# Seven block products for batch 13 of a fused cross-attention kernel, with its statistics later and the loads of x one pair of steps later

## The chip, the cores and the metric

The kernel runs on one core of one Trainium2 chip. The metric is the device time of one execution in microseconds (us), as the median of several runs. All arithmetic is in float32.

## The reference, cut to what matters

There are 16 batches. Each has 256 rows of `x` (256 numbers wide, two tiles of 128 rows) and 77 context rows (192 wide). There are 8 heads of 256.

```
Q = x @ Wq ; K = ctx @ Wk ; V = ctx @ Wv            (8 heads of 256)
score = Q K^T / 16, masked ; attn = softmax(score)   (256 x 77 a head)
out   = concat(attn V) @ Wo + x
return layernorm(out) * gamma + beta                 (over 256 columns)
```

## The kernel before, in words

The kernel never forms Q, K and V. It first multiplies the weights together (`Wk Wq^T` a head into `gA`, `gB`, and `Wv Wo` a head into `uA`, `uB`). For each group of 4 batches it then makes `a` (context times `gA`, `gB`; `prepare_a`, L157) and for each batch `vw` (context times `uA`, `uB`; `prepare_vw`, L205). The scores of a tile are one product of turned `x` with `a`; the output is one product of the turned softmax weights with `vw`.

The work after the start is a hand-written loop over steps `b` from -1 to 14 (L937). Each engine does its instructions strictly in the order in which the code issues them; there is no scheduler. **Step b** holds

- `scores` (L282, TensorE) of the two tiles of batch b+1, then `shift` (L298, VectorE: 16 instructions that add the mask and take the maximum), `exponential` (L318, ScalarE: 16 exponentials), `weigh` (L334, VectorE reciprocal, then GpSimd multiplies into `p`) and `turn` (L352, VectorE transposes `p` into `pT`);
- the output products of batch b;
- the statistics (`finish`, L485: mean and variance on VectorE; `spread`, L507: the inverse root on ScalarE) and the normalisation (`normalise`, L540) of batch b-1, called `old`, and its store. With `aside` the normalisation goes to ScalarE (L546) and GpSimd (L547, L548), and a small GpSimd instruction `less` (L523) goes ahead of it; otherwise it is two VectorE instructions (L533, L552);
- `prepare_vw` and `prepare_a` for later batches, whose results ScalarE copies out of PSUM (L923). Up to step 10 an odd step does this for two batches (a long step, `ahead`) and an even step not at all. From step 11 on every step does it for one.

Tile t belongs to batch t // 2, so tiles 26 and 27 are batch 13.

The output products exist in two forms. `attend` (L362) is eight blocks and a ninth for the last 13 keys, for each tile. `seven(b)` (L421) does the two tiles of a batch at once with seven block products in place of eight (Strassen's scheme in Winograd's form). It needs `differences(b)` (L394: one GpSimd instruction over 768 columns, `ts`) and `sums(b)` (L406: four GpSimd instructions, `ss`, each on the one before or on `pT`), a copy of `pm` to `m` on ScalarE (L459), and afterwards `add_seven(b)` (L462): two additions of `po` to `x` on VectorE (L483) and five additions on GpSimd (L469). `NS` says how many batches take this form: 13 in this kernel, so batches 0 to 12.

The loads are issued by SyncE (SP), also in order: a store waits for its normalisation, and what stands behind it waits too. In odd steps up to 9, `load_x` (L118) brings four tiles of `x` (512 KB, `xg`) and `load_xT` (L144) brings the same four tiles in a blocked order in four transfers of 128 KB (`xT`). Before they are used, `transpose_x` (L154) turns `xT` in place, in two VectorE instructions for four tiles. Here these instructions stand in step b+2 when the loads stand in step b. In an even step the second tile's normalisation is put `behind` and comes in the next step after `shift` and ahead of the loads.

The PSUM has eight banks, taken in turn.

Of the kernel before, what the change touches and what calls it, by code (L numbers as in the profile page):

```python
# [16 lines left out]
P = 128  # L17
# [10 lines left out]
def kernel(  # L28
# [53 lines left out]
    NH = DI // 2 // BK  # L82
    uA = const.tile([P, 5, NH, NF, BK], F32, tag="uA", name="uA")
    uB = const.tile([P, 5, NH, NF, BK], F32, tag="uB", name="uB")
    NS = B - GB // 2 - 1

    def of_e(u, e):
        return u[:, 3 - 2 * e : 5 - 2 * e].rearrange("p q n i c -> p (q n) i c")
# [25 lines left out]
    def load_x(g, n=None, of=QT):  # L114
        if not n:
            xg_of[g] = const.tile([P, GT, DI], F32, tag=f"xg{g}", name=f"xg_{g}")
        lo, hi = (0, GT) if n is None else (n * QT, n * QT + of)
        nc.sync.dma_start(xg_of[g][:, lo:hi], x_rows[:, g * GT + lo : g * GT + hi, :])  # L118
# [3 lines left out]
    def evacuate(dst, src):  # L122
# [3 lines left out]
        else:  # L126
            nc.vector.tensor_copy(dst, src)


    pools = {}  # L130
    xT_of, a_of, vw_of, p_of, mv_of = {}, {}, {}, {}, {}
# [19 lines left out]
    def transpose_x(g, j):  # L151

        cols = xT_of[g][:, j * NM : (j + 2) * NM]
        nc.vector.transpose(cols, cols)  # L154
# [163 lines left out]
    def exponential(t):  # L318
        e = sp.tile([P, H, S2], F32, tag="e", name=f"e_{t}")
        s, top = s_of.pop(t)  # L320
        den = st.tile([P, H], F32, tag="den", name=f"den_{t}")
        for h in range(H):
            one = slice(h, h + 1)
            nc.scalar.activation(  # L324
                e[:, h],
                s[:, h],
                AF.Exp,
                bias=top[:, one],
                scale=-1.0,
                accum_out=den[:, one] if t < QT * NS else None,  # L330
            )
        e_of[t] = e, den

    def weigh(t):  # L334
        e, den = e_of.pop(t)
        if t >= QT * NS:
            nc.vector.tensor_reduce(den, e, AX.X, ALU.add)
        rden = st.tile([P, H], F32, tag="rden", name=f"rden_{t}")
        nc.vector.reciprocal(rden, den)  # L339
        p = p_ring[t % 2]  # L340
        e_mh = e.rearrange("p (m h) k -> p m h k", h=2)
        rden_mh = rden.rearrange("p (m h) -> p m h", h=2)
        for cols, keys in ((slice(2 * KM), slice(KM)), (slice(2 * KM, 2 * S2), slice(KM, None))):
            part = p[:, :, cols].rearrange("p m (h k) -> p m h k", h=2)
            nc.gpsimd.tensor_tensor(  # L345
                part,
                e_mh[:, :, :, keys],
                rden_mh.unsqueeze(3).to_broadcast(list(part.shape)),
                ALU.mult,
            )  # L350

    def turn(t):  # L352
        p = p_ring[t % 2]
        pT_of[t] = turned.tile([P, NF + 1, NM, BK], F32, tag="pT", name=f"pT_{t}", bufs=4)
        nc.vector.transpose(  # L355
            pT_of[t].rearrange("p n m q -> p m n q"),
            p.rearrange("p m (n k) -> p m n k", k=BK),
        )
# [181 lines left out]
    def normalise(t, aside=False, centred=False):  # L540

        g, j = t // GT, t % GT
        rstd, less = rstd_of.pop(t)
        y = xg_of[g][:, j, :]
        if aside:
            nc.scalar.activation(y, y, AF.Identity, bias=less, scale=rstd)  # L546
            nc.gpsimd.tensor_tensor(y, y, gam, ALU.mult)  # L547
            nc.gpsimd.tensor_tensor(y, y, bet, ALU.add)  # L548
        else:
            if not centred:  # L550
                centre(t)
            nc.vector.scalar_tensor_tensor(y, y, rstd, bet, ALU.mult, ALU.add)  # L552
        if t >= NT - 5 * QT:
            store(t)
            return
        done.append(t)
        if t ^ 1 in done:
            t |= 1
            j |= 1
            nc.sync.dma_start(  # L560
                out_rows[:, t + 1 - QT : t + 1, :], xg_of[g][:, j + 1 - QT : j + 1, :]
            )
# [15 lines left out]
    with tc.tile_pool(name="wonce", bufs=1) as wp:  # L578
# [59 lines left out]
            load_blocks(wvT[:, a], wv_blocks[a])  # L638
        for a in range(NF):
            nc.sync.dma_start(wo_of[a // 2][:, a % 2], wo_rows[a])  # L640
        mask_row = mask.rearrange("b k -> (b k)")

        def load_bias(lo, hi):
            nc.sync.dma_start(
                bias_f[:, lo * S2 : hi * S2].bitcast(I32),
                mask_row[lo * S2 : hi * S2].partition_broadcast(P),
            )

        load_xT(0, 0, GT // 2)
        load_bias(0, GB)  # L650
        load_rest()
        load_xT(0, GT // 2, GT)
        load_bias(GB, B)


        idle = ps_mm.tile([P, P], F32, tag="mm", name="idle")
# [194 lines left out]
        for i in range(3):  # L851
            turn_v(i)
        a_of_pairs(2, 3)
        load_x(0)
        nc.sync.dma_start(gam, gamma.partition_broadcast(P))
        nc.sync.dma_start(bet, beta.partition_broadcast(P))
        turn_v(3)
# [52 lines left out]
    def work_of(b, rest_first=False):  # L910
        g, n = b // GB + 1, b % GB
        work = [prepare_vw(b, rest_first)]
        if g < NG - 1 or g == NG - 1 and n < NF // 2:
            work.append(prepare_a(g, (n,), rest_first=rest_first))
        elif b <= NS:
            part = (0, 2) if g < NG else (2, GB)
            work.append(prepare_a(NG - 1, (NF // 2 + n % 2,), *part, rest_first))
        return work
# [5 lines left out]

    behind = []

    def turn_x_and_normalise(g, n, old):
        to_turn = (g, 0) if g < NG and n == 2 else (g - 1, GT // 2) if g > 1 and n == 0 else None
        if to_turn:
            for j in range(to_turn[1], to_turn[1] + GT // 2, 2):  # L930
                transpose_x(to_turn[0], j)
        if old:
            normalise(old[1])

    assert QT == 2
    last = NT - 1
    for b in range(-1, B - 1):  # L937
        old = range(max(b - 1, 0) * QT, b * QT)
        now = range(max(b, 0) * QT, (b + 1) * QT)
        new = range((b + 1) * QT, (b + 2) * QT)  # L940
        for t in new if b >= 0 else ():
            scores(t)
        if b == B - 2:
            for t in old:
                finish(t)
            spread(old[0], old[-1] + 1)
            invert(old[0], old[-1] + 1, aside=old)
            for t in old:
                normalise(t, aside=True)
        for t in new if b >= 0 else ():  # L950
            shift(t)
        while behind:
            behind.pop(0)()
        g, n = (b + 1) // GB + 1, (b + 1) % GB
        if g < NG and n % 2 == 0:
            load_x(g, n, 2 * QT)
            load_xT(g, n * QT, (n + 2) * QT)
        for m in range(0, 2) if b < 0 else range(b + 2, min(b + 3, B // 2)):
            turn_last(m)
        alone = b + 1 >= B - GB  # L960
        works = work_of(b + 1) if alone or n % 2 == 0 else []
        for part_A, _, _ in works:
            part_A()
        for _, part_B, _ in works:
            part_B()
        for i, t in enumerate(new if b >= 0 else ()):
            exponential(t)
            if old and b < B - 2:
                finish(old[i])
            weigh(t)  # L970
        ahead = works and not alone
        if old and b < B - 2 and not ahead:
            spread(old[0], old[-1] + 1)
        if ahead:
            copy_out(works)
            if old:
                spread(old[0], old[-1] + 1)
            works = work_of(b + 2, rest_first=True)
            for _, part_B, _ in works:
                part_B()  # L980
            for part_A, _, _ in works:
                part_A()
        copy_out(works)
        if b + 1 < NS:
            differences(b + 1)
        if b < NS:
            if now:
                seven(b)
            if old:
                invert(old[0], old[-1] + 1)  # L990
                normalise(old[0])
            for t in new:
                turn(t)
            if b < 0:
                for j in range(GT // 2, GT, 2):
                    transpose_x(0, j)
                bias_of(GB, B)
            if alone or ahead:
                turn_x_and_normalise(g, n, old)
            else:  # L1000
                behind.append(partial(turn_x_and_normalise, g, n, old))
            if ahead:
                sums(b + 1)
            if now:
                add_seven(b)
            if b + 1 < NS and not ahead:
                sums(b + 1)
            continue
        for t in now:
            attend(t)  # L1010
        if b < B - 2:
            invert(old[0], old[-1] + 1, aside=old[:1])
            normalise(old[0], aside=True)
            turn(new[0])
            normalise(old[1])
            turn(new[1])
            for t in now:
                add_product(t)
        else:
            turn(new[0])  # L1020
            finish(now[0])
            spread(now[0], now[1])
            turn(new[1])


    attend(last - 1)
# [54 lines left out]
```

## Time and profile before

| what | us |
|---|---|
| median of 3 runs (lowest, highest) | 272.82 (272.69, 273.63) |
| the profiled execution's own time | 272.17 |
| its span in the profile | 270.3 |
| TensorE (PE) busy | 263.6 |
| VectorE (DVE) busy | 185.6 |
| GpSimd (POOL) busy | 171.4 |
| ScalarE (ACT) busy | 155.6 |

The profiled execution lies 0.65 us under the median, and 1.87 us of its time lie outside the span. In the rows below the columns are the start in us, the duration, the engine, the source line and operation, what it writes and reads, and how many instructions were merged; a bracket gives the idle time of the engine before it and what ended it. PEld are TensorE's weight loads, SPq is the queue on which SyncE issues DMAs. The granted clock of TensorE is 1.0 over the whole span after the first microseconds.

Where the steps lie: TensorE begins the scores of step 9 at 188.4, of step 10 at 205.1, of step 11 at 213.2, of step 12 at 225.8, of step 13 at 238.4 and of step 14 at 249.8.

### The profile page before, as it was taken

The page shows a single profiled execution, that of the slowest core. Times are in us where ns is not written, and L with a number is a line of the kernel's source. Part 1 is how long each engine was busy: PE and PEld are TensorE (multiplying, and loading weights), DVE is VectorE, ACT ScalarE, POOL GpSimd, SP SyncE. Part 2 cuts the span into 40 slices and gives each one's busy share as a digit, 9 for nine tenths or more (in the row PEclk, how much of TensorE's full clock was granted, in tenths as well). Part 3 has the DMA queues.
Part 4 walks back from the last instruction along what each step waited for, and adds up shares of the span by engine and source line. Part 5 has one row for each costly group of instructions (what it writes and reads, how often), then busy time and mean ns, then how long its engine had stood idle before and what let it go on. Part 6 is the DMA issues. An engine that isn't in the chain of part 4 may idle for free.

```text
span 270.3 us, 14362 instructions
## 1 busy us (share of the span) xinstructions
PE 263.6 (98%) x6104; PEld 190.5 (70%) x6104; DVE 185.6 (69%) x808; ACT 155.6 (58%) x652; POOL 171.4 (63%) x231
## 2 busy tenths in 40 slices
PE   7999999999999999999999999999999999999993
PEld 6557588754894599449954996489769969684662
DVE  0555938583464858863796479646977898988765
ACT  3233325835858555964687377729584592945752
POOL 1000005726389757996699759964999798966654
PEclk9999999999999999999999999999999999999999
DMA  6998999993000010261016100910091010110102
GB/s 194 203 202 187 327 173 164 309 191 52 2 5 5 2 42 5 75 125 44 2 51 151 41 6 7 191 45 4 7 189 51 2 45 4 44 41 2 62 22 81
DMA packets 42512, 22.69 MB, mean 84 GB/s; under 512 B 23680, under 2 KB 41680, under 8 KB 42448
## 3 DMA queue, kind: packets, MB, share of 16 engines
q1 hardware_dynamic: 42448, 21.77, 37.3%
q8 instruction: 48, 0.79, 1.3%
q14 instruction: 16, 0.13, 0.2%
HBM read 17.57 MB, written 4.19 MB: 81 GB/s over the span
## 4 chain that ended last, share of the span: by engine, by line
PE 91%; DMA 5%; SPq 2%; DVE 1%; issue 0%; DVEq 0%
PE ps L289 25%; PE pa L180 11%; PE pv L214 11%; PE po L434 10%; PE pm L434 9%; PE pv L225 6%; PE pa L192 5%; DMA wk_blk<-in_L_xattn_Wk_dram 5%; PE po L367 4%; PE pu L737 3%; PE pr L248 2%; PE pgb L797 1%; PE pw L751 1%; PE pr L260 1%; SPq L596 1%; PE po L383 1%
## 5 line engine op out<-in xcount | busy, mean ns | idle before, releaser
L324 ACT ACTIVATE e<-s,top 128x77 f32<-128x77 f32 x256 | 83.8, 346 | 46.6 <-DVE top L306 42.6
L289 PE MATMUL ps<-a,xT 128*32 128x154 f32 x2048 | 69.9, 294 | 0.0
L289 PEld LDWEIGHTS ps<-a,xT 128*32 128x32 f32 x2048 | 66.2, 110 | 1.2 <-ACT uB L886 0.4
L345 POOL TENSOR_TENSOR p<-e,rden 128x512 f32<-128x512 f32 x64 | 47.7, 772 | 24.1 <-DVE rden L339 24.1
L306 DVE CUSTOM_DVE_ANT_0 s<-ps,bias 128x77 f32<-128x77 f32 x256 | 43.5, 232 | 15.3 <-PE ps L289 15.3
L324 ACT ACTIVATION_READ_ACCUMULATOR e<-s,top 128x1 f32 x208 | 38.9, 187 | 0.0
L180 PE MATMUL pa<-cA,gA 128*32 128x308 f32 (+1 forms) x576 | 36.4, 394 | 0.0
L469 POOL TENSOR_TENSOR xg<-xg,m 128x256 f32<-128x256 f32 x39 | 28.7, 737 | 7.8 <-DVE xg L483 5.8
L180 PEld LDWEIGHTS pa<-cA,gA 128*32 128x32 f32 x576 | 18.4, 110 | 20.2 <-issue 7.0
L214 PE MATMUL pv<-uA,cA 128*32 128x512 f32 x256 | 30.6, 595 | 0.0
L552 DVE SCALAR_TENSOR_TENSOR xg<-xg,rstd,bet 128x256 f32<-128x256 f32 x26 | 21.2, 816 | 12.8 <-ACT rstd L513 11.5
L398 POOL TENSOR_TENSOR ts<-vw 128x768 f32<-128x768 f32 x13 | 24.0, 1849 | 7.9 <-ACT vw L923 7.9
L355 DVE STREAM_TRANSPOSE pT<-p 128x640 f32<-128x640 f32 x32 | 25.7, 822 | 3.2 <-POOL p L345 3.1
L923 ACT COPY vw<-pv 128x512 f32<-128x512 f32 x32 | 17.7, 584 | 14.7 <-PE pv L214 7.7
L306 DVE DVE_READ_ACCUMULATOR2_ANT top<- 128x1 f32 x256 | 20.8, 81 | 0.0
L483 DVE TENSOR_TENSOR xg<-po,xg 128x256 f32<-128x256 f32 x31 | 11.6, 407 | 13.4 <-PE po L434 12.4
L192 PE MATMUL pa<-cB,gB 64*32 64x308 f32 (+1 forms) x576 | 20.3, 392 | 0.0
L572 POOL TENSOR_TENSOR nan<-nan 128x4 f32<-128x4 f32 (+1 forms) x2 | 0.4, 203 | 31.0 <-DVE nan L571 31.0
L923 ACT COPY a<-pa 128x308 f32<-128x308 f32 (+1 forms) x56 | 18.9, 399 | 1.7 <-PE pa L180 0.2
L192 PEld LDWEIGHTS pa<-cB,gB 64*32 64x32 f32 x576 | 10.7, 107 | 12.3 <-issue 7.5
L225 PE MATMUL pv<-uB,cB 64*32 64x512 f32 x256 | 17.3, 597 | 0.0
L533 DVE SCALAR_TENSOR_TENSOR xg<-xg,mv,gam 128x256 f32<-128x256 f32 x27 | 16.7, 619 | 0.1
(118 smaller groups left out, 409.4 us busy)
## 6 DMA issues: line engine op xcount, KB each, us to landing
xT<-in_x_dram SPq DMA_DIRECT2D x32, 128.0 KB, 5.8
xg<-in_x_dram SPq DMA_DIRECT2D x6, 512.0 KB, 5.0
out_dram<-xg SPq DMA_DIRECT2D x11, 256.0 KB, 2.5
wo<-in_L_xattn_Wo_dram SPq DMA_DIRECT2D x4, 512.0 KB, 6.0
wq_blk<-in_L_xattn_Wq_dram SPq DMA_DIRECT2D x12, 128.0 KB, 4.5
wvT<-in_L_xattn_Wv_dram SPq DMA_DIRECT2D x16, 96.0 KB, 3.4
out_dram<-xg SPq DMA_DIRECT2D x10, 128.0 KB, 2.0
wk_blk<-in_L_xattn_Wk_dram SPq DMA_DIRECT2D x12, 96.0 KB, 4.4
```

Of the source, the lines that this page charges most:

```text
L180: nc.tensor.matmul(flat(o[i * BK : (i + 1) * BK]), gA[:, h, cols(dc, i)], flat(cA[:, batches, :]), start=not rest_first and n in opening, ...
L192: nc.tensor.matmul(flat(banks[j + k][i * BK : (i + 1) * BK]), gB[half(k), h // 2, cols(dc, i)], flat(cB[half(k), batches, :]), start=rest_ ...
L214: nc.tensor.matmul(pv[k][i * BK : (i + 1) * BK], cA[:, b, k * BK : (k + 1) * BK], uA[:, parts, :, i], start=not rest_first, stop=rest_first,)
L225: nc.tensor.matmul(pv[k][i * BK : (i + 1) * BK], cB[half(k), b, k * BK : (k + 1) * BK], uB[half(k), parts, :, i], start=rest_first, stop=n ...
L289: nc.tensor.matmul(ps[m // 2][i * BK : (i + 1) * BK, m % 2 * 2 * S2 : (m % 2 + 1) * 2 * S2], xT_of[g][:, j * NM + m, dc], flat(a_of[g][:, ...
L306: nc.vector.tensor_tensor_reduce(s[:, h], ps[a][:, k * S2 : (k + 1) * S2], bias[:, b, :], scale=-1.0, scalar=FAR, op0=ALU.add, op1=ALU.min ...
L324: nc.scalar.activation(e[:, h], s[:, h], AF.Exp, bias=top[:, one], scale=-1.0, accum_out=den[:, one] if t < QT * NS else None,)
L345: nc.gpsimd.tensor_tensor(part, e_mh[:, :, :, keys], rden_mh.unsqueeze(3).to_broadcast(list(part.shape)), ALU.mult,)
L355: nc.vector.transpose(pT_of[t].rearrange("p n m q -> p m n q"), p.rearrange("p m (n k) -> p m n k", k=BK),)
L434: nc.tensor.matmul(out[i * BK : (i + 1) * BK], weight[:, i], moving, start=first and n == 0, stop=final and n == len(terms) - 1,)
L469: nc.gpsimd.tensor_tensor(to, to, what, ALU.add)
L923: nc.scalar.copy(dst, src)
```

## The change

Batch 13 takes the form with seven products (`NS` is 14). So `differences`, `sums`, `seven` and `add_seven` are issued for it and the two `attend` go. In the last step (14) the statistics and the normalisation of batch 13 stood ahead of the `shift`; `finish` now stands after the first tile's `weigh`, and `spread`, `invert` and `normalise` after the second's.

The loads of `x` and `xT` for a pair of batches stand one pair of steps later, in the same odd step in which `transpose_x` turns them. So step 11 has such loads now, which it had not. In that step the second tile's normalisation stands ahead of `transpose_x`, where it stood after it. At the start, only half of the first group's `x` is loaded early, and the mask's larger part is loaded later. On VectorE the `transpose_x` instructions stay in the same steps as before.

```diff
-    NS = B - GB // 2 - 1
+    NS = B - GB // 2
...
-                accum_out=den[:, one] if t < QT * NS else None,
+                accum_out=den[:, one] if t < QT * (NS - 1) else None,
...
-        load_x(0)
+        load_x(0, 0, 2 * QT)
...
-        elif b <= NS:
+        elif b < NS:
...
-    def turn_x_and_normalise(g, n, old):
-        to_turn = (g, 0) if g < NG and n == 2 else (g - 1, GT // 2) if g > 1 and n == 0 else None
-        if to_turn:
-            for j in range(to_turn[1], to_turn[1] + GT // 2, 2):
-                transpose_x(to_turn[0], j)
+    def normalise_and_turn_x(b, old):
         if old:
             normalise(old[1])
+        coming = (b + 3) * QT
+        if b > 0 and b % 2 and coming < NT:
+            for j in range(coming % GT, coming % GT + 2 * QT, 2):
+                transpose_x(coming // GT, j)
...
-        if b == B - 2:
-            for t in old:
-                finish(t)
-            spread(old[0], old[-1] + 1)
-            invert(old[0], old[-1] + 1, aside=old)
-            for t in old:
-                normalise(t, aside=True)
         for t in new if b >= 0 else ():
             shift(t)
         while behind:
             behind.pop(0)()
         g, n = (b + 1) // GB + 1, (b + 1) % GB
-        if g < NG and n % 2 == 0:
-            load_x(g, n, 2 * QT)
-            load_xT(g, n * QT, (n + 2) * QT)
+        if b < 0:
+            load_bias(GB, B)
+        coming = (b + 3) * QT
+        if b % 2 and coming < NT:
+            load_x(coming // GT, coming % GT // QT, 2 * QT)
+            if b > 0:
+                load_xT(coming // GT, coming % GT, coming % GT + 2 * QT)
...
             weigh(t)
+            if b == B - 2 and t == new[0]:
+                for o in old:
+                    finish(o)
+        if b == B - 2:
+            spread(old[0], old[-1] + 1)
+            invert(old[0], old[-1] + 1, aside=old)
+            for t in old:
+                normalise(t, aside=True)
...
         copy_out(works)
...
         if b < NS:
             if now:
                 seven(b)
+            if b == NS - 1:
+                invert(old[0], old[-1] + 1, aside=old[:1])
+                normalise(old[0], aside=True)
+                turn(new[0])
+                normalise(old[1])
+                turn(new[1])
+                add_seven(b)
+                continue
...
             if alone or ahead:
-                turn_x_and_normalise(g, n, old)
+                normalise_and_turn_x(b, old)
             else:
-                behind.append(partial(turn_x_and_normalise, g, n, old))
+                behind.append(partial(normalise_and_turn_x, b, old))
```

The rest of the diff takes the branch of step 13 out of the code behind the loop's `continue`, and moves `load_bias` up in the file.

## The prediction

> **What bounds the kernel now.** I read the page first: engine totals and the chain of work that ended last.
>
> ```profile
> PE 263.6 (98%) x6104; PEld 190.5 (70%) x6104; DVE 185.6 (69%) x808; ACT 155.6 (58%) x652; POOL 171.4 (63%) x231
> PE 91%; DMA 5%; SPq 2%; DVE 1%; issue 0%; DVEq 0%
> ```
>
> TensorE has work in 263.6 of 270.3 us and is 91% of the chain. Of the 6.7 us left, 1.4 lie before its first matmul and 4.6 after its last (265.7 us). So time is won only by fewer matmuls, and lost wherever another engine lets TensorE wait. Second, windows of the two forms of the product: step 12 with seven, step 13 with two `attend`.
>
> ```profile
> 234.46:238.41 3.95, 3.95 (x135) 3.60 (x133) 3.29 (x6) 2.51 (x8) 3.87 (x7) 1.00 0.12 37
> 245.44:249.78 4.34, 4.34 (x88) 2.63 (x84) 3.88 (x8) 2.06 (x5) 3.57 (x6) 1.00 0.01 4
> ```
>
> The columns after the length are busy time of PE, PEld, DVE, ACT and POOL. Third, the timelines of steps 11 to 13 on VectorE, GpSimd and TensorE, to see how much room stands between a producer and TensorE.
>
> ```profile
> 226.64 1.26 DVE L154 STREAM_TRANSPOSE xT<-xT 128x512 f32<-128x512 f32 x2
> 227.83 0.50 DVE L533 SCALAR_TENSOR_TENSOR xg<-xg,mv,gam 128x256 f32<-128x256 f32 x1
> 228.37 0.56 DVE L552 SCALAR_TENSOR_TENSOR xg<-xg,rstd,bet 128x256 f32<-128x256 f32 x1
> 228.85 0.74 DVE L483 TENSOR_TENSOR xg<-po,xg 128x256 f32<-128x256 f32 x2
> ```
>
> ```profile
> 229.34 2.36 POOL L469 TENSOR_TENSOR xg<-xg,m 128x256 f32<-128x256 f32 x3 [0.69 <-DVE xg L483]
> 231.66 0.74 POOL L415 TENSOR_TENSOR ss<-pT 128x256 f32<-128x256 f32 x1
> 233.17 0.74 POOL L417 TENSOR_TENSOR ss<-pT,ss 128x256 f32<-128x256 f32 x1
> 234.68 3.16 POOL L345 TENSOR_TENSOR p<-e,rden 128x512 f32<-128x512 f32 x4
> 237.80 0.99 POOL L469 TENSOR_TENSOR m<-m 128x128 f32<-128x128 f32 x2
> ```
>
> ```profile
> 234.92 0.62 PE L434 MATMUL pm<-vw,ss 128*32 128x128 f32 x16
> ```
>
> At the end of step 11 GpSimd waits only for VectorE's addition (228.85), then runs without a gap to 238.8. TensorE takes the third of the four sums at 234.92; it was finished at 233.91. That is 1.0 us of room.
>
> **Part 1, the matmuls.** Two `attend` take 4.34 us (second window), seven products 3.95 (first window; 3.92 in step 10, 209.32 to 213.24). TensorE saves 4.34 - 3.93 = 0.41 us in step 13. This is the only gain: all other edits move or add work.
>
> **Part 2, what GpSimd gets.** `differences(13)` 1.85 us (row L398: 1849 ns), `sums(13)` 3.07 us (231.66 to 234.73 in step 12), five additions 3.35 us (237.80 to 238.76 and 240.02 to 242.37). That is 8.3 us in steps 12 to 14, where GpSimd has gaps of 1.2, 2.8 and 1.3 us. Put through in its new order, if nothing before it is late: `p` ends at 237.80, `ts` 239.65, the five additions 243.0 (VectorE's share is ready at 240.27), the sums 246.05, their third at 245.2. TensorE wants that at 245.88: 0.7 us of room, no cost. `p` for tiles 28 and 29 ends at 249.05 (3.0 us), `less` 249.55, ScalarE's pass and two more multiplies for tile 24 end at 251.8 (the same rows take 1.23 and 1.55 us in step 13 now), the five additions of batch 13 at 255.1.
>
> **Part 3, step 14.** The statistics of tiles 26 and 27 now need 255.1. VectorE has the maxima of step 14 ready at 254.55 (now 254.95, less the 0.41 that TensorE is ahead), sums tile 30 until 255.5, then does four statistics (1.09 us), the sum and reciprocal of tile 31 (0.83 + 0.35), so that `p` of tile 31 ends on GpSimd 1.38 us later, at 259.15. Behind it stand in line: `less` (ScalarE can start 0.30 later), two passes on ScalarE, and only then ScalarE's copies of `vw` of batch 15, which were early:
>
> ```profile
> 252.50 1.09 ACT L546 ACTIVATE xg<-xg,less,rstd 128x256 f32<-128x256 f32 x2 [0.40 <-POOL less L523]
> 257.50 1.04 ACT L923 COPY vw<-pv 128x512 f32<-128x512 f32 x2
> ```
>
> The first copy now ends at 259.15 + 0.30 + 1.0 + 0.58 = 261.05. TensorE wants it for tile 30 at 261.16 - 0.41 = 260.75, so it waits 0.3 and 0.1 more for the second copy. The gain of 0.41 is eaten: parts 1 to 3 come to 0.0 us. The same line holds up ScalarE's roots for tiles 28 to 31, which gives the same answer on VectorE's last chain (its addition for tile 30 stays at 263.6).
>
> **Part 4, the loads.** In long steps 3, 5, 7 and 9 the loads and the turning now meet in the same step. The transfers before tell when the last `xT` lands (issue of the last, plus the longest of that step): 121.1, 147.5, 176.7 and 204.9. This is step 9:
>
> ```profile
> L144 SPq DMA_DIRECT2D xT<-in_x_dram x4: 486/492/532, 197.5 to 199.1; - x4
> DMA to landing us min/median/max: 4.5/5.2/5.8
> ```
>
> VectorE, with normalisation put first, comes to the turning at 120.2, 148.0, 176.2 and 203.8. It waits up to 1.1 us, but in steps 3 to 7 it then idles 3 us for TensorE anyway. In step 9 it turns at 204.9 to 206.1, adds 0.7 late and starts the next maxima 0.4 late; the sums for step 11 had 0.3 us of room. Cost 0.1.
>
> **Step 11 is different.** It has only 12.6 us and, until now, no loads. SP's queue: the store waits for the normalisation from `behind` (VectorE, ends 220.58), goes at 220.65, `x` at 221.1. From the issue of `x` to the last `xT` the four steps took 8.9, 7.4, 8.3 and 8.3 us; so it lands at 228.5 to 230.0, mean 229.3. VectorE stands at the turning from 227.8. Behind the waiting instruction are queued: two turnings (1.19), the addition for batch 11 (now 228.85, then 230.55), the 16 maxima of batch 13. So y = 1.7 us late (0.85 to 2.35). GpSimd waits for that addition, and its whole line of part 2 slides by y, as it has no gap left. TensorE then waits in step 12 for the third sum: 1.7 less 1.0 of room = 0.7; in step 13 again 0.3. At the end the statistics come at 255.1 + y, against 255.5 before VectorE would mind: the line to the copies of `vw` ends y - 0.4 = 1.3 us later than in part 3. TensorE's waits in steps 12 and 13 lie inside that 1.3 us, not on top of it: what it loses there it need not wait at the end.
>
> Of that, the queue's price is weighed against a page: the Trainium skill, DMA: Bandwidth & Descriptors, Anatomy of one DMA, gives about 2.0 us fixed plus the bytes at 436 GB/s. By it the 1 MB of these five transfers would take 4.4 us and land at 225.5, no wait, and the sum would be that of part 3 alone. The rows of four steps say 7.4 to 8.9, in pieces of 256 bytes, and I go by them.
>
> **Part 5, the start.** One megabyte less is loaded before 60 us, and the larger mask part comes some 2 us later (it was issued at 43.88 and is used at 61.75). No gap of TensorE lies between 10 and 60 us that a DMA ended. Zero, as 9 us lie between its landing (43.88 + 2 + 6.1 us, the row's time to landing) and its use; without that cover at most the 0.2 us by which the 32 matmuls at 47.95 (3.26) are longer than those at 54.11 (3.03).
>
> **Sum.** -0.4 (matmuls) + 0.4 (copies of `vw` late) + 1.3 (line from step 11) = +1.3 us: a span of 271.6, a profiled run of 273.5, a median of 272.82 + 1.3 = 274.1. About 0.5% (1.36 us) is what a measurement of this kernel can tell from no change, so this forecast lies on the edge. With y from 0.85 to 2.35 the end moves by 0.45 to 1.95: 273.3 to 274.8.
>
> **Rivals.** *The loads are in time* (not slower). If the last `xT` of step 11 lands by 228.0 (6.9 us after the issue of `x`, quicker than any of the four rows) or GpSimd's line has 1 us of slack that I don't see, parts 1 to 3 alone hold: 272.4 to 272.9, and 272.4 if the copies of `vw` are in time too. For it speaks the spread of 1.5 us between four equal steps; against it, that none of the four was so quick. *VectorE and GpSimd stretch each other* (slower still). The same VectorE row L552 takes 0.48 us alone and up to 1.09 beside GpSimd, a sum 0.74 or 0.92. If the five slid GpSimd stages of steps 12 to 14 each pay 0.2 to 0.3, and step 9's transfer is as late as step 3's (8.9: another 0.6 on TensorE in step 11), the end moves by 2.4 to 3.2: 275.2 to 276.0. It decides as soon as GpSimd's `ss` in step 13 start after 246. *The change doesn't do what it says*: no; on TensorE 40 matmuls of 256 columns become 56 of 128 and 8 of 256 in the built order.
>
> **How the numbers follow.** Line from step 11: 0.66, of that half on each side of 274.18. Loads in time: 0.20. Stretch: 0.14. Faster by over 0.5% (under 271.5) would need three times the saved matmuls: 0.03, from the first rival. Within 0.5%: 0.17 + 0.33 = 0.50. Slower: 0.33 + 0.14 = 0.47. The range 272.7 to 275.4 leaves out the faster half of the first rival and the worse half of the second.
>
> **What would show it.** Right: in step 11 VectorE waits 1 to 2 us for DMA at `xT`; GpSimd's wait at `xg` there grows from 0.7 to over 2; TensorE shows gaps before `pm<-vw,ss` in steps 12 and 13 and before `po` of tile 30; that product of step 13 takes 3.9 us. Wrong: no wait of VectorE for `xT` in step 11, or TensorE without gaps up to its end; or a wait in the long steps that reaches TensorE.

## Result, and the profile after

The changed kernel takes 275.0 us (median of 11 runs, 273.94 to 275.84) against 272.82 us for the kernel before: a ratio of 1.0074, 95% interval 1.0054 to 1.0093, so slower by 2.2 us. A second set of runs gave 275.36 against 272.85 us, ratio 1.010 (1.0073 to 1.0128). The forecast was 274.1 us, with a range of 272.7 to 275.4: right in sign and, in the main, in mechanism, and 0.9 us short. The profiled execution took 274.31 us with a span of 272.4 us (before: 272.17 and 270.3). Lines of code lie some 8 further down: what was L469 is L477, L533 is L541.

The engine totals and the chain by engine, from the page of the changed kernel:

```profile
PE 264.1 (97%) x6152; PEld 191.3 (70%) x6152; DVE 188.4 (69%) x808; ACT 156.1 (57%) x653; POOL 179.8 (66%) x241
...
PE 72%; DVE 10%; DMA 6%; POOL 3%; SPq 3%; ACT 3%; issue 1%; DVEq 0%; POOLq 0%
```

GpSimd is busy for 8.4 us more; part 2 counted 8.3. TensorE was 91% of the chain and is 72%: the chain now runs through a transfer, VectorE and GpSimd. The windows of the seven products of step 12 and of step 13 (length, then busy time of PE, PEld, DVE, ACT, POOL):

```profile
234.66:239.58 4.92, 4.15 (x133) 3.54 (x132) 4.60 (x10) 4.13 (x15) 4.76 (x6) 1.00 0.01 3
246.62:251.13 4.51, 4.15 (x137) 3.54 (x133) 3.25 (x9) 3.01 (x10) 4.35 (x7) 1.00 0.01 4
```

Before, step 12 took 3.95 us from the first product to the next step's scores; now 4.92. Step 13's seven take 4.51, longer than the two `attend` they replace (4.34). Why they do is in the timelines. VectorE at the end of step 11 (start, duration, and in brackets the idle time ahead of it with what ended it):

```profile
227.10 1.27 DVE L541 SCALAR_TENSOR_TENSOR xg<-xg,mv,gam 128x256 f32<-128x256 f32 x1
228.41 0.56 DVE L560 SCALAR_TENSOR_TENSOR xg<-xg,rstd,bet 128x256 f32<-128x256 f32 x1
229.78 1.31 DVE L162 STREAM_TRANSPOSE xT<-xT 128x512 f32<-128x512 f32 x2 [0.80 <-DMA xT<-in_x_dram]
231.00 0.71 DVE L491 TENSOR_TENSOR xg<-po,xg 128x256 f32<-128x256 f32 x2
```

VectorE stands at the turning until the last `xT` lands, and the addition behind it comes at 231.00 instead of 228.85. Then GpSimd, and the product of TensorE that needs the third sum, in steps 12 and 13:

```profile
231.47 2.37 POOL L477 TENSOR_TENSOR xg<-xg,m 128x256 f32<-128x256 f32 x3 [2.18 <-DVE xg L491]
...
235.30 0.72 POOL L425 TENSOR_TENSOR ss<-pT,ss 128x256 f32<-128x256 f32 x1
```

```profile
236.07 0.65 PE L442 MATMUL pm<-vw,ss 128*32 128x128 f32 x16 [0.77 <-POOL ss L425]
...
247.62 0.65 PE L442 MATMUL pm<-vw,ss 128*32 128x128 f32 x16 [0.36 <-POOL ss L425]
```

GpSimd starts 2.13 us later than before (229.34) and TensorE waits, where it had 1.0 us of room in step 12. The brackets count only idle time. From the first product of the batch to this second one it is 1.41 us in step 12 (from 234.66) and 1.00 us in step 13 (from 246.62), where the kernel before took 0.46 (234.46 to 234.92); so the product comes 0.95 and 0.54 us late. By the same measure it is 0.23 us late in step 11 already, too little for a bracket: first the kernel before, then the changed one, and the third sum that it waits for.

```profile
221.88 0.65 PE L434 MATMUL pm<-vw,pT 128*32 128x128 f32 x16
222.34 0.62 PE L434 MATMUL pm<-vw,ss 128*32 128x128 f32 x16
```

```profile
221.82 0.64 PE L442 MATMUL pm<-vw,pT 128*32 128x128 f32 x16
222.51 0.65 PE L442 MATMUL pm<-vw,ss 128*32 128x128 f32 x16
```

```profile
221.72 0.73 POOL L425 TENSOR_TENSOR ss<-pT,ss 128x256 f32<-128x256 f32 x1
```

The transfers of step 11 by their line (shortest, median and longest of the four issues on SP in ns, and the time to landing):

```profile
L152 SPq DMA_DIRECT2D xT<-in_x_dram x4: 551/728/1422, 222.1 to 224.8; - x4
...
DMA to landing us min/median/max: 4.9/5.9/6.0
```

Last, ScalarE in step 14, and VectorE's last two normalisations:

```profile
260.98 1.10 ACT L554 ACTIVATE xg<-xg,less,rstd 128x256 f32<-128x256 f32 x2 [2.15 <-POOL less L531]
261.99 1.04 ACT L922 COPY vw<-pv 128x512 f32<-128x512 f32 x2
```

```profile
266.22 0.96 DVE L541 SCALAR_TENSOR_TENSOR xg<-xg,mv,gam 128x256 f32<-128x256 f32 x1
...
268.51 0.64 DVE L541 SCALAR_TENSOR_TENSOR xg<-xg,mv,gam 128x256 f32<-128x256 f32 x1
```

The copies of `vw` now end 9.4 us before the end instead of 11.8, behind `less` and two passes. Both normalisations took 0.48 us before; GpSimd's multiplies now lie beside them.

### The profile page after: what moved, and what is told of

Same layout as the page of the kernel before. It is cut to its first block, busy times and chain, and to the rows that moved or that the text cites. A ratio compares the mean times of both kernels' runs of the same rounds, so it can differ in the third digit from the quotient of the medians.

```text
span 272.4 us, 14475 instructions
## 1 busy us (share of the span) xinstructions
PE 264.1 (97%) x6152; PEld 191.3 (70%) x6152; DVE 188.4 (69%) x808; ACT 156.1 (57%) x653; POOL 179.8 (66%) x241
## 4 chain that ended last, share of the span: by engine, by line
PE 72%; DVE 10%; DMA 6%; POOL 3%; SPq 3%; ACT 3%; issue 1%; DVEq 0%; POOLq 0%
PE ps L297 20%; PE pa L188 10%; PE po L442 9%; PE pv L222 8%; PE pm L442 7%; PE pa L200 5%; DMA wk_blk<-in_L_xattn_Wk_dram 5%; PE pv L233 4%; PE pu L736 3%; PE pr L256 2%; DVE s L314 2%; DMA xT<-in_x_dram 2%; DVE xg L541 2%; ACT e L332 1%; PE pgb L796 1%; POOL p L353 1%
## 5 line engine op out<-in xcount | busy, mean ns | idle before, releaser
L477 POOL TENSOR_TENSOR xg<-xg,m 128x256 f32<-128x256 f32 x42 | 30.9, 735 | 8.2 <-DVE xg L491 5.9
L406 POOL TENSOR_TENSOR ts<-vw 128x768 f32<-128x768 f32 x14 | 25.8, 1844 | 7.9 <-ACT vw L922 7.9
L541 DVE SCALAR_TENSOR_TENSOR xg<-xg,mv,gam 128x256 f32<-128x256 f32 x27 | 19.7, 729 | 0.1
```

Of the source, the lines that this page charges most:

```text
L406: nc.gpsimd.tensor_tensor(ts.rearrange("p q k d -> p q (k d)"), vw[:, 1:4], vw[:, 0:1].to_broadcast([P, 3, 2 * P]), ALU.subtract,)
L477: nc.gpsimd.tensor_tensor(to, to, what, ALU.add)
```

## Experiments

Two numbers are given for each. The first is the median, against that of the kernel before on the same chip (272.74 us for seven_alone, loads_alone, last_loads_in_step_10 and last_turning_in_step_12; 272.72 for last_loads_in_step_10_again, extra_transfers, xT_before_x and seven_alone_copies_first; 272.85 for the other four). The second is the traced execution's time from the first product `pm<-vw,pT` of step 1 to the end of the span, because the start of the kernel alone varies by over 2 us from one execution to the next (in these traces the step-0 product starts between 72.9 and 75.7 us). By that measure before is 177.57 (270.3 - 92.73) and the changed kernel 179.73 (272.4 - 92.67): 2.16 us more.

**seven_alone: the seven products and late statistics without the later loads.** The edit: in the changed kernel, the loads, those of the start too, and the turnings go back to where they were.

```diff
-        if b % 2 and coming < NT:
-            load_x(coming // GT, coming % GT // QT, 2 * QT)
...
+        if g < NG and n % 2 == 0:
+            load_x(g, n, 2 * QT)
+            load_xT(g, n * QT, (n + 2) * QT)
```

> The seven products for batch 13 and the late statistics of step 14, with loads, turnings and their order as in the kernel before. Theory (the late turning in step 11 is the loss): -0.4 us of matmuls against +0.4 us of late copies of vw, so 272.5 to 273.1 us, no change; GpSimd's first three additions of step 11 start near 229.3 again. Rival (GpSimd's 8.3 us of new work and the late statistics are the loss): 274.3 to 275 us with these loads too, and TensorE waits for the sums in steps 12 and 13.

272.94 us, ratio 1.0007 (0.9989 to 1.0025); 177.65 in the trace, 0.08 more than before. Its view of waits names none of TensorE after the start. The seven products, GpSimd's 8.3 us of new work and the late statistics come to nothing together: parts 1 to 3 are 0.0, as forecast, and the rival that blamed them falls. What each of them gives and takes is in the last two experiments.

**loads_alone: the later loads without the seven products.** The edit is made in the kernel before; the later loads at the start go with it.

```diff
-    def turn_x_and_normalise(g, n, old):
+    def normalise_and_turn_x(b, old):
...
+        if b % 2 and coming < NT:
+            load_x(coming // GT, coming % GT // QT, 2 * QT)
```

> The later loads and the turning behind the normalisation, with two attend products for batch 13 and the early statistics as in the kernel before. Theory: VectorE's addition of step 11 comes near 231.0 (2.1 us late), TensorE waits 1.0 us for the third sum in step 12 and 0.25 in step 11, and with no sums of batch 13 it waits for nothing more: 273.8 to 274.4 us. Rival (seven products are the loss): no wait in step 12 because GpSimd has room, 272.6 to 273.1 us.

274.31 us, ratio 1.0064 (1.0041 to 1.0088); 179.23, 1.66 more than before. So the loads carry most of the loss, but the trace shows it in two places. TensorE's timeline:

```profile
227.65 4.00 PE L297 MATMUL ps<-a,xT 128*32 128x154 f32 x116 [0.72 <-issue]
...
237.03 0.65 PE L442 MATMUL pm<-vw,ss 128*32 128x128 f32 x16 [0.34 <-POOL ss L425]
```

The second is the wait expected, only smaller; the first, in the middle of the scores, waits for nothing that the profile shows. Neither theory had it.

**last_loads_in_step_10: the wait of step 11 taken away.** The five transfers are issued a step earlier, the turning stays.

```diff
-        if b % 2 and coming < NT:
+        if b == 10:
+            coming = (b + 4) * QT
+        if (b % 2 and b < 11 or b == 10) and coming < NT:
```

> The changed kernel, only the five transfers of step 11 are issued in step 10; the turning stays in step 11. Theory: VectorE's wait for xT in step 11 goes, its addition comes at 229 to 229.7, TensorE's waits for the third sum in steps 12 and 13 fall to 0 to 0.3 and what is left is step 9's 0.25 and part 3: 272.8 to 273.4 us. Rival (VectorE and GpSimd stretch each other, or the seven products themselves): the waits in steps 12 and 13 stay over 0.5 each, 274.3 to 275 us.

274.42 us, ratio 1.0077 (1.005 to 1.0105); 179.51, 1.94 more than before. VectorE no longer waits for `xT` in step 11, and TensorE no longer for the sums in steps 12 and 13 (under 0.15 us), yet little or nothing is won (the changed kernel's ratios are 1.0074 and 1.010). In the place of those waits the timeline of TensorE has, while the transfers are in flight:

```profile
212.58 0.73 PE L297 MATMUL ps<-a,xT 128*32 128x154 f32 x16 [1.14 <-issue]
```

My expectation missed by over 1 us. The new question was what holds TensorE there.

**last_loads_in_step_10_again: the same kernel, a second trace.**

> The same kernel as last_loads_in_step_10, for a second trace. If the 1.14 us gap in the scores of step 11 comes from the fetch of instructions behind the transfers, it is there again, at the same matmul, 0.5 to 1.3 us long, and TensorE's waits in steps 12 and 13 are again under 0.1. If it was a chance of one execution, it is gone and the span from the first seven products to the end is under 198 us (before: 197.35).

One run, 273.93 us; 179.10. The gap is there again, but 256 instructions further on; VectorE's turning of step 11 again starts without a wait:

```profile
213.86 0.38 PE L442 MATMUL po<-vr,pT 128*32 128x256 f32 x1 [0.50 <-issue]
```

```profile
228.99 1.29 DVE L162 STREAM_TRANSPOSE xT<-xT 128x512 f32<-128x512 f32 x2
```

Counted in the trace, TensorE had begun 9409 instructions (weight loads, matmuls and semaphore instructions) when it stopped the first time, 9665 in this trace and 10433 in loads_alone: each time 193 more than a multiple of 256. The trace has packets of 16,384 bytes on an instruction queue, one for about every 256 instructions of TensorE, and in each of the three the gap ends 1.41 to 1.45 us after such a packet lands. It isn't "the same matmul" that I expected, but the same place in a block of instructions. The place comes back, the matmul doesn't, and a packet has just landed each time: TensorE waits for its own code.

**extra_transfers: the transfers alone.** The kernel before, with the same five transfers in step 11 into a tile that is no longer read.

```diff
+        if b == B - 5:
+            load_unread()
...
+        nc.sync.dma_start(unread[...], x_rows[:, lo : lo + 2 * QT, :])
+        for i in range(NM):
+            nc.sync.dma_start(unreadT[i * BK : (i + 1) * BK]..., rows[i])
```

> The kernel before, and in step 11 five more transfers of the same form and size as the changed kernel's (512 KB and four of 128 KB), into a tile that nobody reads any more. Nothing waits for them and no instruction of another engine is added. Theory now (beside the late turning, the transfers in flight hold up the fetch of TensorE's instructions, as the two gaps of 0.72 and 1.14 us that the chain names issue suggest): in some executions a gap of 0.3 to 1.2 us before a matmul within 10 us after the issue, with no releaser, and the median 0.2 to 0.8 us over before: 272.9 to 273.6 us. Rival (transfers that nobody waits for are free): 272.6 to 272.9 us and no such gap.

274.29 us, ratio 1.0052 (1.0025 to 1.008); 179.17, 1.60 more than before, above the upper end that I expected. Of the 1.60 us, 1.44 lie between the first products of steps 11 and 12 (222.59 to 236.61; before 221.88 to 234.46). No instruction of another engine was added and nothing waits for these bytes. TensorE's timeline, then the queues between 222 and 228 us (packets, MB, share of 16 engines):

```profile
228.21 4.00 PE L304 MATMUL ps<-a,xT 128*32 128x154 f32 x116 [1.13 <-issue]
```

```profile
q1 hardware_dynamic: 2830, 1.29, 101.0%
q8 instruction: 1, 0.02, 1.2%
```

The gap is at instruction 10433 again, 193 over. The data queue fills all 16 DMA engines for these 6 us, and the one packet of code among them lands 4.14 us after the first product of step 11 (226.73 against 222.59), where in before it lands 2.25 us after it (224.13 against 221.88). The gap ends 1.48 us after the landing.

**extra_x_alone and extra_xT_alone: half of it each.** From extra_transfers, the four transfers are left out for the first, the one for the second.

```diff
 (extra_x_alone)
-            nc.sync.dma_start(unreadT[i * BK : (i + 1) * BK]..., rows[i])
 (extra_xT_alone)
-        nc.sync.dma_start(unread[...], x_rows[:, lo : lo + 2 * QT, :])
```

> The kernel before, and in step 11 only the unread transfer of 512 KB of x (pieces of 1 KB). If the fetch of instructions is held up in proportion to what is queued ahead of it, half the bytes hold it up half as long, and as TensorE has some hundred instructions in hand, under half the loss is left: 272.8 to 273.4 us. If any transfer at that place costs the same, 274.0 to 274.5 us.

> The kernel before, and in step 11 only the four unread transfers of 128 KB in pieces of 256 bytes. If the number of pieces counts and not the bytes, this costs most of what all five cost: 273.6 to 274.3 us; if the bytes count, as little as the 512 KB of x alone: 272.8 to 273.4 us.

272.94 us (1.0004, 0.9986 to 1.0023) and 273.25 us (1.0023, 0.9997 to 1.005): neither can be told from before, while both together cost 1.6 us. By the medians, half the bytes cost under half, in large pieces or in small (for the small ones the interval reaches 1.4 us). The numbers don't tell pieces from bytes, as the two intervals overlap. The one trace of extra_x_alone has 178.51, 0.94 more than before, and what it lost is code again: TensorE stops for 0.2 to 0.4 us between two starts at instructions 9153, 9409 and 10433, each 193 over a multiple of 256, too short for a bracket. The first two cost 0.59 us between the first products of steps 9 and 10, where the kernel before has loads of its own and nothing was added. So these stops come and go with the execution. Counted at one packet to 256 instructions, in no trace of this case does an instruction at such a place start less than 1.26 us after its packet lands, and where the packet lands over 2 us ahead, TensorE goes on at its usual pace: it has code in hand, and only a delay that outlasts it is paid.

**last_turning_in_step_12: another head of the line.** In the changed kernel the two turnings of step 11 go behind the maxima of step 12.

```diff
-            if alone or ahead:
+            if b == B - 5:
+                normalise(old[1])
+                behind.append(partial(normalise_and_turn_x, b, ()))
+            elif alone or ahead:
```

> The changed kernel, only the two turnings of step 11 are done in step 12, after its maxima; the loads stay in step 11. Theory (the waiting instruction at the head of VectorE is the loss, not the lateness of the data): VectorE's addition of step 11 comes near 228.2, GpSimd starts 2.5 to 3 us earlier than in the changed kernel, no wait of TensorE in steps 12 and 13: 272.6 to 273.3 us. Rival (the data's lateness counts, or VectorE has no room in step 12 for 1.2 us more): 274 to 275 us, the wait only moves into step 12.

273.86 us, ratio 1.0035 (1.0015 to 1.0054); 178.02, 0.45 more than before. VectorE's timeline, then GpSimd's:

```profile
229.25 0.74 DVE L491 TENSOR_TENSOR xg<-po,xg 128x256 f32<-128x256 f32 x2
...
232.44 1.29 DVE L162 STREAM_TRANSPOSE xT<-xT 128x512 f32<-128x512 f32 x2
```

```profile
229.74 2.35 POOL L477 TENSOR_TENSOR xg<-xg,m 128x256 f32<-128x256 f32 x3
```

The same loads, as late as in the changed kernel, and TensorE waits in neither step 12 nor step 13: the waiting instruction at the head of VectorE was what those waits came from, and VectorE has room for it in step 12. Of the change's 2.16 us, 1.7 are gone in the trace. The median is 0.6 us over the range expected, more than its one trace explains; this trace has no gap of 0.1 us for code, so what the other executions had is open.

**xT_before_x: the order on the queue.** The edit is in the changed kernel, for every pair.

```diff
-            load_x(coming // GT, coming % GT // QT, 2 * QT)
             if b > 0:
                 load_xT(coming // GT, coming % GT, coming % GT + 2 * QT)
+            load_x(coming // GT, coming % GT // QT, 2 * QT)
```

> The changed kernel, only in each pair's loads the four transfers of xT go ahead of the 512 KB of x. Theory (the turning waits for the last xT, and that is set by five transfers in line on one queue): without 512 KB ahead of it the last xT of step 11 lands 0.5 us (one issue) to 2.5 us (a bandwidth share) earlier, 227.3 to 229.3; VectorE's addition of step 11 at 229 to 230.5, TensorE's wait in step 12 0 to 0.7: 273.2 to 274.5 us. Rival (only the issues count): 229.3 and over, 274.4 to 274.9 us.

273.28 us, ratio 1.0017 (0.999 to 1.0043); 178.39. By its landing events the last `xT` of step 11 is there at 228.29, and VectorE doesn't wait:

```profile
228.70 1.29 DVE L162 STREAM_TRANSPOSE xT<-xT 128x512 f32<-128x512 f32 x2
```

That is 6.9 us after the first issue (221.37), against 8.2 us from the issue of `x` (221.56) to the turning in the changed kernel. TensorE's wait in step 12 is gone, and of the one in step 13 0.3 us are left (the product with the third sum starts at 246.57, 0.77 us after the first product). The order alone wins back most of the loss (273.28 against 275.0 and 275.36 us in other sets of runs).

**changed_again: the changed kernel, a second trace.**

> The changed kernel itself, for a second trace and another median beside the others. Both theories in one: the late turning costs 0.8 to 1.4 us in every execution (TensorE's waits for the third sum in steps 12 and 13), and the late fetch of instructions comes on top in some executions only. So VectorE's addition of step 11 comes again at 230.5 to 231.5 in the trace, a gap named issue of 0 to 1.2 us may or may not be in it (within 10 us after the loads of step 11), and the median is 274.6 to 275.4 us.

275.36 us; 179.88, 2.31 more than before. VectorE, then TensorE:

```profile
230.61 1.31 DVE L162 STREAM_TRANSPOSE xT<-xT 128x512 f32<-128x512 f32 x2 [1.03 <-DMA xT<-in_x_dram]
```

```profile
236.91 0.64 PE L442 MATMUL pm<-vw,ss 128*32 128x128 f32 x16 [0.99 <-POOL ss L425]
...
248.47 0.65 PE L442 MATMUL pm<-vw,ss 128*32 128x128 f32 x16 [0.38 <-POOL ss L425]
```

The same two waits as in the first trace, and again no gap named issue of 0.1 us in TensorE. In neither trace of the changed kernel is the loss one of code; the late turning carries it. What its other executions had can't be seen.

**seven_alone_copies_first and seven_alone_reordered: where the 0.4 us of saved matmuls go.** Both start from seven_alone. The first puts the copies of `vw` of batch 15 (`copy_out`) ahead of the late roots, `less` and passes, at the start of the block `if b == B - 2`; the second is this edit, with the roots and `less` ahead of `p` of tile 31 and the copies behind them:

```diff
+            if b == B - 2 and t == new[1]:
+                spread(old[0], old[-1] + 1)
+                invert(old[0], old[-1] + 1, aside=old)
             weigh(t)
...
         if b == B - 2:
-            spread(old[0], old[-1] + 1)
-            invert(old[0], old[-1] + 1, aside=old)
+            copy_out(works)
+            works = []
```

> seven_alone, and in step 14 ScalarE's copies of vw of batch 15 ahead of the roots and normalisation of tiles 26 and 27. Theory (part 3: the copies behind the late statistics give back the 0.4 us that the seven products save): no wait of TensorE before po of tile 30, PE's last matmul 0.3 to 0.4 us earlier against its start, 272.4 to 272.7 us, 0.2 to 0.5 under seven_alone. Rival (the end is set by VectorE's and ScalarE's last chains, not by the copies): the same time as seven_alone within 0.15 us.

> seven_alone, and in step 14 the roots of tiles 26 and 27 and their two less ahead of p of tile 31 (on ScalarE and GpSimd), then the copies of vw, then the two normalisation passes. Theory (with the copies early, the end is set by the line p of tile 31, less, ScalarE's passes, GpSimd's multiplies, which stretch VectorE's last normalisation from 0.48 to 0.90 us): the passes start 0.8 to 1.5 us earlier, the last normalisation takes 0.5 us, and the end comes 0.3 to 0.5 us earlier after the first seven products than in seven_alone: 272.3 to 272.7 us. Rival (something else on VectorE's last chain is as late): as seven_alone within 0.15 us.

Copies first: 272.94 us, as seven_alone; 177.61 (seven_alone: 177.65). TensorE's last matmul ends 0.16 us earlier after step 12's first product than in seven_alone (237.22 to 268.05, against 235.59 to 266.58), not the 0.3 to 0.4 that I expected, and the stretch from there to the end of the span stays near 5 us (268.05 to 273.1; before 265.68 to 270.3, 4.6 us). Reordered: 272.35 us, ratio 0.9983 (0.996 to 1.0006); 177.19, 0.38 less than before and 0.46 less than seven_alone, and the stretch behind TensorE is back at 4.63. VectorE's last normalisation, first in copies_first, then in reordered:

```profile
269.02 0.90 DVE L541 SCALAR_TENSOR_TENSOR xg<-xg,mv,gam 128x256 f32<-128x256 f32 x1
```

```profile
267.04 0.48 DVE L541 SCALAR_TENSOR_TENSOR xg<-xg,mv,gam 128x256 f32<-128x256 f32 x1
```

So the rival held for the first and the theory for the second: the copies are only one branch of the line behind `p` of tile 31; its other branch, `less`, ScalarE's passes and GpSimd's multiplies, sets the end. Of the 0.4 us of saved matmuls, seven_alone gives back 0.16 in TensorE's waits for the copies, and the rest and a little more in the stretch behind TensorE. The reordered kernel is the best of all here: faster than the changed one by 3.0 us in the same set of runs (272.35 against 275.36), and faster than before in the trace by the 0.4 us of part 1, which the timing can't tell from no change.

## Why the prediction was right, point by point

**Parts 1 to 3** held: 0.0 forecast, +0.1 to +0.2 measured (seven_alone). The term of the copies (+0.4) was right in sum and wrong in its place: TensorE gave back only 0.16 us waiting for them, and without these waits the end stays where it is. The sentence that the same line "gives the same answer on VectorE's last chain" is what the two reorderings showed.

**Part 4, step 11** was the mechanism: the wait at `xT` (0.80 and 1.03 us in the two traces), GpSimd's wait at `xg` (2.18 us), the third sums that reach TensorE too late in steps 12 and 13 (brackets of 0.77 and 0.36, and 0.99 and 0.38; the product itself 0.95 and 0.54 us late in the first trace; forecast 0.7 and 0.3). Mis-sized was y: 2.15 us (231.00 - 228.85) instead of 1.7, inside its 0.85 to 2.35. The time from the issue of `x` to the turning was as the four steps gave it, 8.2 us; but the issue came at 221.56 instead of 221.1. The price from the Trainium skill, DMA: Bandwidth & Descriptors, Anatomy of one DMA (landing at 225.5) didn't hold: the last transfer, issued at 224.8, took 4.9 us and landed 4 us later than that. The page gives its formula for one DMA on GpSimd's path; these were five, issued by SyncE.

**Step 9** was the term that failed most in proportion: forecast 0.1. VectorE waited 1.14 us there in the first trace, its addition came 0.9 us late (206.26 instead of 205.38), and that lateness ran on through step 10. It was paid twice. In step 11 the third sum ended at 222.45, and TensorE took it 0.23 us late; so a wait in a long step did reach TensorE, which the prediction had named as a sign against it (in the second trace it is 0.01). And the store and the loads behind it in step 11 started 0.5 us late (221.11 and 221.56). That steps 3 to 7 cost nothing held: from step 0 to the first product of step 11 TensorE's intervals from product to product are those of before to 0.01 us.

**The line to the end**, "y - 0.4", was not what bound TensorE. Its products with the third sum are 0.23, 0.95 and 0.54 us late, together 1.7 us, and after the first product of step 11 TensorE ends 1.8 us later than in seven_alone. At `po` of tile 30, where the prediction had the copies of `vw` set the end, it waits 0.10 us (262.60 instead of 262.50), as in seven_alone (0.09). So TensorE's waits for the sums were the cost itself and not a part of the 1.3 us. The 0.9 us that the forecast is short are found in the sum for the whole trace: from step 1's first product TensorE ends 1.6 us later than before (forecast 1.3), and the stretch behind it is 0.6 us longer (5.20 against 4.62; forecast 0). Half of these 0.6 are the late statistics, which seven_alone has too (4.92). The rest goes with ScalarE's pass for tile 30, which waits for a later instruction of VectorE than in seven_alone, so that GpSimd's last addition lies beside VectorE's last normalisation (0.64 us instead of 0.48). Seven_alone, then last_turning_in_step_12:

```profile
266.66 0.51 ACT L1042 ACTIVATE xg<-xg,rstd 128x256 f32<-128x256 f32 x1 [0.53 <-DVE xg L541]
```

```profile
266.37 0.51 ACT L1048 ACTIVATE xg<-xg,rstd 128x256 f32<-128x256 f32 x1 [0.80 <-DVE xg L509]
```

The late turning isn't its cause, since last_turning_in_step_12 has no late addition in step 11 and the same 0.64. Why the built program waits there isn't shown.

**Part 5, the start,** can't be read off: the start varies by over 2 us between executions. The losses from step 1 on account for those of the medians, so no cost is needed there, and one of a few tenths isn't excluded.

**The signs.** VectorE's wait fell short of the 1 us named in the first trace (0.80), because VectorE itself came to the turning late. GpSimd's wait and TensorE's gaps in steps 12 and 13 came. The one before `po` of tile 30 didn't, and the product of step 13 takes 4.51 us and not 3.9, as its wait lies inside it.

**The rivals.** *Loads in time* didn't happen, but xT_before_x made its condition nearly true (228.29 for 228.0) and came 0.4 us above its times (273.28). *Stretch* was half there: the normalisation in step 11 took 1.27 us instead of 0.50 beside GpSimd, but ended 0.8 us before the transfer did; and the `ss` of step 13 started at 245.34, short of the 246 from which it was to decide. (Its row L552 takes up to 1.75 us in the kernel before, at 88.95, not 1.09.)

**Not in the prediction at all** was that the transfers hold up TensorE's code. It didn't show in the two traces of the changed kernel, so the forecast didn't need it; but it is why the remedy that the prediction implies, the same loads a step earlier, wins little or nothing. The two losses don't add: in loads_alone a gap of 0.72 us makes TensorE late itself, and the wait for the sum shrinks to 0.34.

## What to carry to other kernels

Look at what stands behind the instruction that waits for a transfer: moving that instruction, or putting the transfers that it waits for first on the queue, won back over 1 us by the medians here, with the same bytes loaded in the same step. A transfer that nobody waits for isn't free: cost a dense burst also by what shares the DMA engines, and read a gap named issue in TensorE's timeline against the packets of the instruction queue. When work off the critical engine is postponed, follow every branch of its line to the end before taking one of them for the bound.

## What was not expected of the hardware

TensorE stopped for its instructions. In four traces gaps of 0.50 to 1.14 us by the timeline stand at 193 instructions over a multiple of 256, and end 1.41 to 1.48 us after a 16,384-byte packet lands on the instruction queue, while 1 MB of loads was in flight. Shorter stops at such places are in the trace of extra_x_alone, and one of 0.22 us at 61.56 in that of seven_alone_copies_first. The Trainium skill, Runtime: NRT & Kernel Launch, Instruction fetch mechanics, has blocks of 16 KiB or 256 instructions, fetched ahead by the engine's own queue at a cost that is mostly hidden. The block agrees with the 193 that come back; hidden it was not, where a burst of five transfers met the fetch: 1.57 us on the median in extra_transfers.
